# A last block product that accumulates onto U3, with new tile counts and scheduler margins, in a four-layer graph network on one core

## The chip, the cores and the metric

The kernel runs on one core of one Trainium2 chip. The metric is the device time of one execution in microseconds. The core has five engines that run side by side: TensorE (PE, matmuls; PEld is its weight load), VectorE (DVE), ScalarE (ACT), GpSimd (POOL) and SyncE (SP), whose queue here issues all transfers between memory and the on-chip buffers. Matmul results go to PSUM, which has eight banks; DVE and ACT read them from there.

## What is computed

Four graph layers follow one another, each closed by a residual sum and a layer norm. All data are fp32; `x` is 128 graphs x 64 nodes x 512 features. Cut to what matters:

```python
# layer 0
y = x @ w;  s = y @ a
A = s[..., :, None] + s[..., None, :];  A = tanh(A / 8) * 8;  A = where(A >= 0, A, 0.1 * A)
A = exp(A) * adj;  A = A / A.sum(-1) * adj.sum(-1)
x = layernorm(x + A @ x @ w)
# layer 1
weight = adj * exp(query @ key.T);  x = layernorm(x + weight / weight.sum(2) @ value)
# layer 2
w = scale * mask * sum(q * (adj @ k), -1);  x = layernorm(x + softmax(w) * (x @ Wv))
# layer 3
h = layernorm(relu(hypergraph_conv(x, adj, W1, b1)));  x = layernorm(x + hypergraph_conv(h, adj, W2, b2) + x)
```

`hypergraph_conv` multiplies by the weights and gathers along the graph's edges twice. What costs time are the dense products with weight matrices of 512x512 (layers 0 to 2), 512x1024 and 1024x512 (layer 3), for 8192 rows.

## The kernel before

**Tiling.** The 8192 rows are cut into 64 tiles of 128 rows, two graphs in each; two tiles make a group (`GT`), so there are 32 groups, and two groups make a pair (`SG`). Work inside one graph (gathers, scores) uses TensorE divided into 64x64 or 128x64 tiles, since a graph has 64 nodes; products with weights use the whole array.

**Seven products instead of eight.** Each dense product is done by a Strassen-Winograd scheme on 2x2 blocks. Of the left side A, sums s0 to s3 are made on DVE (`side_sums`); of the weights B, sums t1 to t4 are made once (`combine`) and stored. The order in which the seven right sides are stored and streamed is `USE` (L516). `products_of` (L949 on) does seven products in two standing PSUM banks (0 and 1) and two further banks: bank 0 takes A11 B11, then s1 t2 on top of it, which gives U2; then s2 t3 on top, which gives U3. Bank 1 takes s0 t1 and then s3 B22. A12 B21 and A22 t4 each go to a bank of their own. `first` moves a bank to the result block, `more` adds it to one; the callers give both as functions (`scaled_into`, `plain_into`, `z_into`, and a pair inside `run_rest`). C22 takes U3, and C21 is U3 plus the product A22 t4, taken from its own bank.

**Seven times seven.** The first weight product of layer 3 does the scheme on two levels (`forty_nine_products`, L1097), for a pair of groups at a time. `inner_products` (L1053) does one inner seven in two banks `x_` and `y_`: `times` issues a product, `into` moves columns of a bank into the result tile `f`. `use` adds the outer results into the blocks of h.

**Buffers.** Tiles are of few kinds with a fixed number each (L326 on): `x` 7 (activations of a group), `k4` 14 (left sides, sums and intermediate results of 1024 columns), `ring` 8 (weights on the way in), `adj` 10, `kept` 9, `e` 7, `col` 40, `bank` 8 (PSUM). Two kinds hold no memory and only limit how many are under way: `product` 3 (sevens) and `inner` 2.

**Order of the work.** Nothing runs in the order in which it is written. Every operation is recorded with its engine, an estimated cost, what it reads and writes, and a key (`Order.add`). `Order.run` is a list scheduler: it walks an own clock, and on each engine starts the ready operation with the smallest key whose tiles are free. The resulting order of each engine is then emitted and pinned; on the chip, engines wait for one another by semaphores. So all instructions have line L1471. Constants steer it:

- `BASE`, `EARLY`, `LEAD`, `PREPARED`: keys of groups, steps and the preparation of weights;
- `LATENCY`, `TO_PE`: how long after an operation's end another engine is taken to see it; for PE, `TO_PE` comes on top;
- `TURN`, `FAR`, `NEAR`, `ENOUGH` in `choose`: when PE is turned between the whole array ("whole") and a divided one ("quarters", "columns");
- `BLOCK`, `REST`: a divided matmul is let in only if the one 64 matmuls earlier began at least `REST` ns before;
- `AHEAD`, `TOGETHER`: how far transfers may run ahead, and how strongly the pieces of one weight are asked for together.

Of the kernel before, what the change touches and what calls it, by code (L numbers as in the profile page):

```python
# [28 lines left out]
APART = 4  # L29

BASE = [
    0.0, 1.743, 3.111, 5.432, 10.971, 14.755, 19.549, 23.249, 27.849, 31.549, 36.149, 39.849, 44.449, 48.149, 52.749, 56.449,
    61.049, 64.749, 69.349, 73.049, 77.649, 81.349, 85.949, 89.649, 94.249, 97.949, 102.549, 106.249, 111.542, 113.859, 117.859, 118.633,
]
RESIDENT = ("m1", "m2")
APART_3A = (0, NG // SG - 1)
LEAD = [0.325, -0.58]
PREPARED = [-5.214, 7.399, 8.218, 12.615, 11.711, -0.62]
PIECE = 1024
EPS = 1e-5  # L40
TINY = 1.1754944e-38
# [26 lines left out]
class Order:  # L68
    LATENCY = {"PE": 210, "DVE": 125, "ACT": 140, "POOL": 120, "SP": 2200}
    AGAIN = {"PE": 0, "DVE": 115, "ACT": 115, "POOL": 120}  # L70
    TO_PE = 100
    BYTES_PER_NS = 300
    UNDERWAY = 8
    TURN, TURN_DIVIDED = 145, 60

    NEAR = 0.5
    FAR = 5.712
    ENOUGH = 48

    EARLY = [2.22, 0.626, 0.0, 0.0, 0.0, -0.394, 0.0, 1.328, 0.0, 0.456, -0.17, -0.03, -0.766, -0.36, -1.408, -0.964]  # L80

    BLOCK, REST = 64, 3500
    AHEAD = 3.5
    TOGETHER = 1.0

    def __init__(self, slots):
        self.slots = {kind: list(range(n))[::-1] for kind, n in slots.items()}
# [200 lines left out]
def kernel(  # L288
# [34 lines left out]
    def kind(name, n, *shape, space=None):  # L323
        kinds[name] = [(space or sbuf).tile([P, *shape], FP, name=f"{name}{i}") for i in range(n)]

    kind("x", 7, GT, D)  # L326
    kind("k4", 14, PIECE)
    kind("ring", 8, PIECE)
    kind("h", 2, GT, DH)
    kind("k2", 2, D)  # L330
    kind("adj", 10, CT, N)
    kind("kept", 9, CT, N)
    kind("bh", 2, CT, N + 2)
    kind("e", 7, GT, N)
    kind("col", 40, 16)
    kind("bank", 8, D, space=psum)
    kinds["product"] = [None] * 3
    kinds["inner"] = [None] * 2

    order = Order({k: len(v) for k, v in kinds.items()})  # L340

# [171 lines left out]

    USE = ("b11", "t1", "b21", "t2", "b22", "t4", "t3")  # L516
    HALF = PIECE // 2

    def combine(b, t, n):
# [429 lines left out]
    def products_of(sides, pieces, across=False):  # L949


        going = Buf("product")
        pairs = [[Buf("bank") for _ in range(2)] for _ in sides]
        deep, wide = ("deep" in sides[0][0], "wide" in sides[0][0])
        chunks = KH // 2 if deep else KC // 2
        width = PIECE // chunks if deep or wide else D // 2
        pieces = iter(pieces)

        def times(of, ps, left, piece, view, start=True, also=(), gate=()):
            token = pairs[of][ps] if isinstance(ps, int) else ps  # L960

            def emit():
                l, b, o = left[1](), view(), token.t
                if across:
                    for c in range(2):
                        for k in range(chunks):
                            nc.tensor.matmul(o[:, ts(c, P)], b[:, k, ts(c, P)], l[:, k, :],
                                             start=start and k == 0 and c == 0,
                                             stop=k == chunks - 1, skip_group_check=True)
                else:  # L970
                    for k in range(chunks):
                        nc.tensor.matmul(o[:, :width], l[:, k, :], b[:, k, :], start=start and k == 0,
                                         stop=k == chunks - 1, skip_group_check=True)

            pe(w_pe(P, 2 * chunks) if across else w_pe(width, chunks), [left[0], piece, going, *gate], [token, *also], emit,
               matmuls=2 * chunks if across else chunks)
            return (token, going), lambda: token.t[:, :width]

        def all_times(ps, left, start=True, opens=False):
            piece, view = next(pieces)  # L980
            for of, (a, s, first, more) in enumerate(sides):
                yield first, more, times(of, Buf("bank") if ps is None else ps, left(a, s), piece, view, start,
                                         *(at_once if opens and of == 0 else ()))

        at_once = [b for pair in pairs[1:] for b in pair], [side[1][i][0] for side in sides[1:] for i in range(4)]
        for first, more, p in all_times(0, lambda a, s: a["11"], opens=True):
            first("11", *p)
        for first, more, p in all_times(1, lambda a, s: s[0]):
            first("22", *p)
        for first, more, p in all_times(None, lambda a, s: a["12"]):  # L990
            more("11", *p)
        for first, more, p in all_times(0, lambda a, s: s[1], False):
            first("12", *p)
        for first, more, p in all_times(1, lambda a, s: s[3], False):
            more("12", *p)
        for first, more, p in all_times(None, lambda a, s: a["22"]):
            first("21", *p)
        for first, more, p in all_times(0, lambda a, s: s[2], False):
            more("22", *p)
            more("21", *p)  # L1000

    def block_views(b, view):

# [8 lines left out]
    def scaled_into(at, f, own, n, sums):  # L1012


        def add(k, token, ps, last):
            dst = at[k]
            t = own.start + int(k[0]) - 1
            c = 2 * (int(k[0]) - 1) + int(k[1]) - 1
            dve(n + 40 + 70 * last, [*token, f, dst[0]], [dst[0], *([sums[c]] if last else [])], lambda: nc.vector.scalar_tensor_tensor(
                dst[1](), ps(), f.t[:, t : t + 1], dst[1](), ALU.mult, ALU.add,  # L1020
                **({"accum_out": sums.t[:, c : c + 1]} if last else {})), NOW)

        return lambda k, token, ps: add(k, token, ps, False), lambda k, token, ps: add(k, token, ps, True)

    def plain_into(b):

# [26 lines left out]
    def inner_products(raw, room, at, which, pieces, f, width):  # L1053


        going, x_, y_ = Buf("inner"), Buf("bank"), Buf("bank")
        raw_tok, raw_view = raw

        def side(k):
            if k in KEYS:  # L1060
                return raw_tok, lambda: raw_view(k)
            return room[int(k)], lambda: at(int(k))[:, which]

        def times(bank, i, k, start=True):
            piece, view = next(pieces)
            token, left = side(k)

            def emit():
                nc.tensor.matmul(bank.t[:, ts(i, width)], left(), view()[:, 0], start=start, stop=True, skip_group_check=True)

            pe(w_pe(width), [token, piece, going], [bank, *([y_] if k == "11" else [])], emit, matmuls=1)

        def into(cells, bank, i, n=1, first=False):
            n *= width
            dst = lambda: f.t[:, cells[0] * width : cells[0] * width + n]
            src = lambda: bank.t[:, i * width : i * width + n]
            if first:
                act(n, [bank], [f[cells]], lambda: nc.scalar.copy(dst(), src()), NOW)
            else:
                dve(n, [bank, f[cells]], [f[cells]], lambda: nc.vector.tensor_add(dst(), src(), dst()), NOW)  # L1080

        times(x_, 1, "11")
        times(x_, 0, "0", False)
        into([1, 2], x_, 0, 2, True)
        times(y_, 0, "12")
        times(x_, 1, "1", False)
        times(x_, 0, "3", False)
        into([0], x_, 1, 1, True)
        into([0], x_, 0)
        times(y_, 1, "22", False)  # L1090
        times(x_, 1, "2", False)
        into([3], x_, 1, 1, True)
        into([1], x_, 1)
        into([2, 3], y_, 0, 2)


    def forty_nine_products(xT, a, s, pieces, width, use):  # L1097
# [28 lines left out]
            return (of["tokens"], lambda k: of[k]()[:, m]), room, at, m  # L1126

        pieces = iter(pieces)
        for name in ("1", "5", "2", "6", "3", "4", "7"):
            raw, room, at, m = prepared_side(name)  # L1130
            f = Buf("k4", 4)
            inner_products(raw, room, at, m, pieces, f, width)
            use(name, f)
# [213 lines left out]
    def run_rest(n):  # L1347
# [15 lines left out]
        def h_block(r, j):  # L1363
            return hs[r][block_cells(j)], lambda: hs[r].t.rearrange("p t d -> p (t d)")[:, ts(j, DH)]
# [14 lines left out]
        def use(name, f_):  # L1379
            f = kept[name] = f_, lambda: f_.t  # L1380
            if name == "2":
                add(h_block(0, 0), kept["1"], f)
            elif name == "6":
                add(f, kept["1"], f, pool)
                add(h_block(0, 1), f, kept["5"])
            elif name == "3":
                add(h_block(0, 1), h_block(0, 1), f)
            elif name == "7":
                add(f, kept["6"], f, pool)
                add(h_block(1, 0), f, kept["4"])  # L1390
                add(h_block(1, 1), f, kept["5"])

        def by_part(v):
            return v.rearrange("p (i n) -> p i n", n=DH // 4)
# [147 lines left out]
```

## Time and profile before

| | |
|---|---|
| median of 3 runs | 2155.4 us (2155.09 to 2163.58) |
| profiled execution | 2158.28 us, its span 2156.5 us |
| granted TensorE clock | 0.997 |
| matmul records on PE | 21427 |
| ring<-3a, loads of 512 KB | 196, 4.9 us from issue to landing |
| ring<-v, loads of 512 KB | 189, 3.6 us from issue to landing |

The span is the time from the first to the last instruction of one profiled execution. Names of tiles stand without their numbers: `bank<-ring,k` is a matmul of a weight in `ring` with a left side in a `k` tile, `bank<-k,m` one with the weights that stay on the chip, `bank<-kept,h`, `bank<-kept,x`, `bank<-e,x` and `bank<-k,e` are the products inside graphs. A shape such as `128*128 128x256` gives the part of the array and then the output. An fp32 matmul leaves two records on PE and two weight loads on PEld; a transpose leaves one of each. DVE reads banks in these groups:

```profile
L1471 DVE SCALAR_TENSOR_TENSOR x<-bank,col,x 128x256 f32<-128x256 f32 x768 | 355.3, 480 | 274.9 <-PE bank L1471 259.1 <-issue 7.9 <-ACT k L1471 4.7
L1471 DVE TENSOR_TENSOR k<-bank,k 128x256 f32<-128x256 f32 x580 | 233.9, 420 | 161.0 <-PE bank L1471 112.0 <-ACT k L1471 42.5 <-ACT x L1471 0.5
...
L1471 DVE TENSOR_TENSOR k<-bank,k 128x512 f32<-128x512 f32 x98 | 66.8, 684 | 13.6 <-PE bank L1471 9.8 <-ACT k L1471 3.3
```

A row of groups gives the line, engine and operation, then out<-in, the shapes and the count; after the bar the busy time in us and the mean of one in ns; after the second bar the idle time before them and what ended most of it.

### The profile page before, as it was taken

The page shows a single profiled execution, that of the slowest core. Times are in us where ns is not written, and L with a number is a line of the kernel's source. Part 1 is how long each engine was busy: PE and PEld are TensorE (multiplying, and loading weights), DVE is VectorE, ACT ScalarE, POOL GpSimd, SP SyncE. Part 2 cuts the span into 40 slices and gives each one's busy share as a digit, 9 for nine tenths or more (in the row PEclk, how much of TensorE's full clock was granted, in tenths as well). Part 3 has the DMA queues.
Part 4 walks back from the last instruction along what each step waited for, and adds up shares of the span by engine and source line. Part 5 has one row for each costly group of instructions (what it writes and reads, how often), then busy time and mean ns, then how long its engine had stood idle before and what let it go on. Part 6 is the DMA issues. An engine that isn't in the chain of part 4 may idle for free.

```text
span 2156.5 us, 53957 instructions
## 1 busy us (share of the span) xinstructions
PE 2118.2 (98%) x21427; PEld 1833.8 (85%) x21427; DVE 1480.0 (69%) x4346; ACT 1195.4 (55%) x2698; POOL 457.5 (21%) x434
## 2 busy tenths in 40 slices
PE   8999999999999999999999999999999999999998
PEld 4897788888888898888888888898888888888875
DVE  5766876675686857668586685867768586765754
ACT  2544755464564645557464574645657365664554
POOL 1211330212211212121122211122121221212220
PEclk9999999999999999999999999999999999999999
DMA  8788873663655546456463555536465454645455
GB/s 270 257 310 288 298 268 116 219 212 116 204 177 209 188 147 212 144 205 209 162 204 135 200 191 200 193 127 228 152 209 194 170 198 136 209 161 186 159 189 184
DMA packets 166315, 422.36 MB, mean 196 GB/s; under 512 B 34928, under 2 KB 52528, under 8 KB 166064
## 3 DMA queue, kind: packets, MB, share of 16 engines
q1 hardware_dynamic: 166064, 418.92, 57.5%
q8 instruction: 169, 2.77, 0.5%
q14 instruction: 82, 0.67, 0.1%
HBM read 382.77 MB, written 36.08 MB: 194 GB/s over the span
## 4 chain that ended last, share of the span: by engine, by line
PE 95%; DMA 2%; ACT 1%; issue 1%; DVE 1%; SPq 0%; POOLq 0%; DVEq 0%; ACTq 0%
PE bank L1471 95%; DMA ring<-v 1%; ACT k L1471 1%; DMA adj<-mask_rows 1%; DVE k L1471 0%; ACT h L1471 0%; SPq L1471 0%; DMA ring<-3a 0%; DMA k<-in_wk_dram 0%; DVE x L1471 0%; DVE col L1471 0%; ACT e L1471 0%; ACT x L1471 0%; DVE ring L1471 0%; ACT m L1471 0%
## 5 line engine op out<-in xcount | busy, mean ns | idle before, releaser
L1471 PE MATMUL bank<-ring,k 128*128 128x256 f32 (+1 forms) x4940 | 1185.8, 388 | 7.9 <-ACT k L1471 4.8
L1471 PEld LDWEIGHTS bank<-ring,k 128*128 128x128 f32 x4940 | 903.3, 190 | 163.7 <-issue 22.9
L1471 ACT COPY k<-bank 128x512 f32<-128x512 f32 (+1 forms) x934 | 425.6, 483 | 425.5 <-PE bank L1471 370.1
L1471 DVE SCALAR_TENSOR_TENSOR x<-bank,col,x 128x256 f32<-128x256 f32 (+1 forms) x832 | 398.9, 500 | 277.8 <-PE bank L1471 261.8
L1471 PEld LDWEIGHTS bank<-k,m 128*128 128x128 f32 x3584 | 435.1, 192 | 15.2 <-ACT k L1471 2.4
L1471 PE MATMUL bank<-k,m 128*128 128x128 f32 x3584 | 442.7, 275 | 0.0
L1471 DVE TENSOR_TENSOR k<-bank,k 128x256 f32<-128x256 f32 (+1 forms) x678 | 295.0, 459 | 174.7 <-PE bank L1471 121.8
L1471 ACT ACTIVATE k<-x,col 128x512 f32<-128x512 f32 x256 | 183.9, 720 | 244.5 <-DVE col L1471 232.6
L1471 POOL TENSOR_TENSOR col<-col,mhalf 128x2 f32<-128x2 f32 (+1 forms) x161 | 111.6, 694 | 950.3 <-DVE col L1471 419.0
L1471 ACT ACTIVATE x<-x,col,col 128x512 f32<-128x512 f32 x256 | 198.4, 812 | 67.0 <-DVE col L1471 66.9
L1471 PE MATMUL bank<-ring,h 128*128 128x256 f32 x1024 | 233.0, 380 | 0.0
L1471 PEld LDWEIGHTS bank<-ring,h 128*128 128x128 f32 x1024 | 192.0, 190 | 26.3 <-issue 1.0
L1471 DVE TENSOR_TENSOR k<-k 128x256 f32<-128x256 f32 (+1 forms) x349 | 151.6, 454 | 47.0 <-ACT k L1471 44.2
L1471 DVE TENSOR_TENSOR k<-k,k 128x256 f32<-128x256 f32 (+3 forms) x361 | 174.4, 494 | 0.8
L1471 POOL TENSOR_TENSOR x<-x,bv_b 128x512 f32<-128x512 f32 x64 | 81.7, 1285 | 262.1 <-DVE col L1471 198.9
L1471 POOL TENSOR_TENSOR k<-k,b3b_b 128x512 f32<-128x512 f32 x64 | 80.4, 1270 | 201.2 <-DVE k L1471 148.2
L1471 PEld LDWEIGHTS bank<-k,k 128*64 128x64 f32 (+1 forms) x2112 | 77.9, 140 | 39.3 <-issue 27.0
L1471 PE MATMUL bank<-k,k 128*64 128x64 f32 (+1 forms) x2112 | 105.6, 238 | 5.5 <-DMA k<-in_wk_dram 5.1
L1471 ACT ACTIVATE k<-bank,u_c 128x128 f32<-128x128 f32 x256 | 85.9, 366 | 42.1 <-PE bank L1471 40.5
L1471 POOL TENSOR_TENSOR k<-k,k 128x1024 f32<-128x1024 f32 (+1 forms) x31 | 72.0, 2323 | 141.8 <-DVE k L1471 107.7
L1471 DVE TENSOR_TENSOR h<-k,k 128x1024 f32<-128x1024 f32 (+1 forms) x88 | 89.9, 1025 | 16.8 <-POOL k L1471 8.2
L1471 DVE TENSOR_SCALAR col<-col 128x2 f32<-128x2 f32 (+2 forms) x402 | 78.7, 199 | 24.4 <-ACT k L1471 18.0
(102 smaller groups left out, 1628.9 us busy)
## 6 DMA issues: line engine op xcount, KB each, us to landing
ring<-3a SPq DMA_DIRECT2D x196, 512.0 KB, 4.9
ring<-v SPq DMA_DIRECT2D x189, 512.0 KB, 3.6
ring<-3b SPq DMA_DIRECT2D x126, 512.0 KB, 4.6
ring<-w SPq DMA_DIRECT2D x93, 512.0 KB, 4.2
x<-in_x_dram SPq DMA_DIRECT2D x32, 512.0 KB, 6.3
ring<-v SPq DMA_DIRECT2D x63, 256.0 KB, 4.3
out_dram<-x SPq DMA_DIRECT2D x31, 512.0 KB, 6.4
ring<-w SPq DMA_DIRECT2D x31, 256.0 KB, 4.7
```

Of the source, the lines that this page charges most:

```text
L1471: made = f(*args, **kwargs)
```

## The change

The order of the last two products of a seven is exchanged, at both levels. s2 t3 makes U3 in bank 0, and `more` adds it to C22. Then A22 t4 accumulates in the same bank on top of U3, which makes C21 there, and `first` moves it. Before, C21 was written from the bank of A22 t4 and U3 was added to it. So one move out of PSUM is left out in each seven, and the last product has to wait until U3 has been read. In the inner sevens the bank `y_` now holds one product instead of two, and in `use` the block C21 of the outer level is the sum of results 4 and 7. `USE` and the streaming order follow. In `scaled_into` the running sum for the layer norm is taken by the write to C21 as well, since it is now the block's last.

Beside this the tile counts and the scheduler's constants are changed.

```diff
 BASE = [
-    0.0, 1.743, 3.111, 5.432, 10.971, 14.755, 19.549, 23.249, 27.849, 31.549, 36.149, 39.849, 44.449, 48.149, 52.749, 56.449,
...
+    0.0, 1.743, 3.111, 5.372, 10.971, 14.755, 18.98, 22.38, 27.28, 30.68, 35.58, 38.98, 43.88, 47.28, 52.18, 55.58,
...
-LEAD = [0.325, -0.58]
-PREPARED = [-5.214, 7.399, 8.218, 12.615, 11.711, -0.62]
+LEAD = [2.505, -0.294]
+PREPARED = [-3.906, 7.537, 8.271, 13.522, 12.862, -0.62]
...
-    TO_PE = 100
+    TO_PE = 300
...
-    FAR = 5.712
-    ENOUGH = 48
-
-    EARLY = [2.22, 0.626, 0.0, 0.0, 0.0, -0.394, 0.0, 1.328, 0.0, 0.456, -0.17, -0.03, -0.766, -0.36, -1.408, -0.964]
-
-    BLOCK, REST = 64, 3500
-    AHEAD = 3.5
-    TOGETHER = 1.0
+    FAR = 6.79728
+    ENOUGH = 28.88843999999999
+
+    EARLY = [2.22, 0.626, 0.0, -0.759, 0.0, -0.394, 0.0, 1.328, 0.0, 1.09, 0.384, -0.03, -0.766, -0.36, -1.408, -0.964]
+
+    BLOCK = 64
+    REST = 4500
+    AHEAD = 4.2
+    TOGETHER = 0.7
...
-    kind("x", 7, GT, D)
-    kind("k4", 14, PIECE)
+    kind("x", 6, GT, D)
+    kind("k4", 18, PIECE)
...
-    kind("adj", 10, CT, N)
-    kind("kept", 9, CT, N)
+    kind("adj", 6, CT, N)
+    kind("kept", 6, CT, N)
...
-    kind("e", 7, GT, N)
-    kind("col", 40, 16)
+    kind("e", 4, GT, N)
+    kind("col", 28, 16)
     kind("bank", 8, D, space=psum)
-    kinds["product"] = [None] * 3
-    kinds["inner"] = [None] * 2
+    kinds["product"] = [None] * 2
+    kinds["inner"] = [None] * 3
...
-    USE = ("b11", "t1", "b21", "t2", "b22", "t4", "t3")
+    USE = ("b11", "t1", "b21", "t2", "b22", "t3", "t4")
...
-        for first, more, p in all_times(None, lambda a, s: a["22"]):
-            first("21", *p)
         for first, more, p in all_times(0, lambda a, s: s[2], False):
             more("22", *p)
-            more("21", *p)
+        for first, more, p in all_times(0, lambda a, s: a["22"], False):
+            first("21", *p)
...
-        return lambda k, token, ps: add(k, token, ps, False), lambda k, token, ps: add(k, token, ps, True)
+        return lambda k, token, ps: add(k, token, ps, k == "21"), lambda k, token, ps: add(k, token, ps, True)
...
-        times(y_, 1, "22", False)
+        into([2], y_, 0)
         times(x_, 1, "2", False)
-        into([3], x_, 1, 1, True)
         into([1], x_, 1)
-        into([2, 3], y_, 0, 2)
+        times(x_, 1, "22", False)
+        into([3], x_, 1, 1, True)
...
-        for name in ("1", "5", "2", "6", "3", "4", "7"):
+        for name in ("1", "5", "2", "6", "3", "7", "4"):
...
-                add(h_block(1, 0), f, kept["4"])
                 add(h_block(1, 1), f, kept["5"])
+            elif name == "4":
+                add(h_block(1, 0), f, kept["7"])
```

More of the change, by code (lines that the diff above doesn't have):

```diff
@@ L31 @@
 BASE = [
-    0.0, 1.743, 3.111, 5.432, 10.971, 14.755, 19.549, 23.249, 27.849, 31.549, 36.149, 39.849, 44.449, 48.149, 52.749, 56.449,
-    61.049, 64.749, 69.349, 73.049, 77.649, 81.349, 85.949, 89.649, 94.249, 97.949, 102.549, 106.249, 111.542, 113.859, 117.859, 118.633,
+    0.0, 1.743, 3.111, 5.372, 10.971, 14.755, 18.98, 22.38, 27.28, 30.68, 35.58, 38.98, 43.88, 47.28, 52.18, 55.58,
+    60.48, 63.88, 68.78, 72.18, 77.08, 80.48, 85.38, 88.78, 93.68, 97.08, 101.98, 105.38, 110.213, 112.471, 117.658, 118.432,
 ]
@@ L1089, in inner_products @@
         into([0], x_, 0)
-        times(y_, 1, "22", False)
+        into([2], y_, 0)
         times(x_, 1, "2", False)
+        into([1], x_, 1)
+        times(x_, 1, "22", False)
         into([3], x_, 1, 1, True)
-        into([1], x_, 1)
-        into([2, 3], y_, 0, 2)
     def forty_nine_products(xT, a, s, pieces, width, use):
```

## The prediction

> **What bounds the kernel now.** First the page: busy shares, and the chain that ended last.
>
> ```profile
> PE 2118.2 (98%) x21427; PEld 1833.8 (85%) x21427; DVE 1480.0 (69%) x4346; ACT 1195.4 (55%) x2698; POOL 457.5 (21%) x434
> ...
> PE 95%; DMA 2%; ACT 1%; issue 1%; DVE 1%; SPq 0%; POOLq 0%; DVEq 0%; ACTq 0%
> ```
>
> TensorE is busy for 98% of 2156.5 us and carries 95% of the chain. The vector engine, from which the change takes work, idles for 31% and holds 1% of the chain. So I ask only what the change does to the stream of matmuls. What could still be saved there is next, in the waits of PE:
>
> ```profile
> PE bank L1471 <- issue: 12.8, 9, 3.7
> PE bank L1471 <- DMA k<-in_wk_dram: 5.1, 1, 5.1
> PE bank L1471 <- ACT k L1471: 4.9, 5, 1.9
> PE bank L1471 <- ACT e L1471: 4.5, 3, 3.7
> ```
>
> The largest item, nine stops of 12.8 us, waits for no buffer and no engine. The others stand at the start and the end. Waits under 0.15 us are not listed, so I read the timeline of PE; one stretch gives nearly all prices:
>
> ```profile
> 999.49 0.81 PE L1471 MATMUL bank<-ring,k 128*128 128x256 f32 x3
> 1000.24 1.15 PE L1471 MATMUL bank<-k,k 128*64 128x64 f32 x32
> 1001.32 1.16 PE L1471 MATMUL bank<-kept,h 64*64 64x64 f32 x64
> 1002.41 1.13 PE L1471 MATMUL bank<-ring,k 128*128 128x256 f32 x4
> 1003.38 0.28 PE L1471 MATMUL bank<-row_of,e 128*128 128x2 f32 x2
> ...
> 1010.43 1.63 PE L1471 MATMUL bank<-kept,h 64*64 64x64 f32 x96
> 1011.99 0.70 PE L1471 MATMUL bank<-ring,k 128*128 128x256 f32 x2
> ```
>
> Starts are to be compared, not durations, since matmuls overlap. A record on the whole array (128*128, 256 columns) starts 0.216 us after the one before. From whole to divided the start comes at 1000.24 instead of 999.49 + 3 x 0.216 = 1000.14: 0.10 lost. 64 records on 64*64 tiles last 1.09 to the next whole matmul, 96 last 1.56: 0.47 for 32, so 1.09 holds 0.15 that is no work. The next whole matmuls need 0.97 for four (0.86 of work): 0.10 more. One trip from whole to divided and back costs 0.35 us, a step between two divided shapes 0.15.
>
> Now a stop:
>
> ```profile
> 1263.50 1.09 PE L1471 MATMUL bank<-k,e 64*64 64x512 f32 x8
> 1264.41 1.46 PE L1471 MATMUL bank<-kept,h 64*64 64x64 f32 x88
> 1266.91 0.34 PE L1471 MATMUL bank<-kept,h 64*64 64x64 f32 x8 [1.03 <-issue]
> ```
>
> Eight records of one group come 1.25 us after the 88 before them. The DMA part of the page says what is fetched there:
>
> ```profile
> q8 instruction: 169, 2.77, 0.5%
> ```
>
> 169 packets of 16 KB bring PE's 42,854 recorded instructions, some 254 each: 64 fp32 matmuls of four instructions. The 128 matmul records before this stop began within 3.8 us; with the stop the block took 5.1. A block of 64 matmuls that is done faster than about 5 us outruns its fetch.
>
> And a short wait:
>
> ```profile
> 975.42 1.05 PE L1471 MATMUL bank<-k,m 128*128 128x128 f32 x8
> 976.51 0.70 PE L1471 MATMUL bank<-ring,k 128*128 128x256 f32 x2
> ```
>
> Eight records at 0.112 end at 976.32; the next starts 0.19 late, behind an addition of DVE, and the one after it 0.10 late again.
>
> **What the skill says.** TensorEngine Tiling (Array Packing), Key Properties: changing the tiling mode drains TensorE. The trace agrees: 0.35 us a trip. Runtime: NRT & Kernel Launch, Instruction fetch mechanics: instructions come in blocks of 256, the next fetched while one runs, the cost mostly hidden. The block size agrees; hidden it is not in nine places. TensorE: Matmul & The Clock Gate, Step-by-step: matmuls keep program order, only weight loads are pulled ahead, so a matmul that waits holds every later one. PSUM — Partial Sum Buffer, The four PSUM rules: a synchronised read in the middle of an accumulation group is allowed, which the new last link needs. The first bank of the kernel before is already read that way, so the trace has the case.
>
> **The change, part by part.** I compared the order that the two sources give on each engine.
>
> *Evacuations.* Removed on DVE: 96 scaled additions (128x256, 480 ns: 46 us), 96 plain ones (420 ns: 40 us), and 98 of 512 columns (684 ns) that shrink to 256 (26 us). DVE falls by some 112 us, ACT stays. On the path this is worth nothing: DVE's idle 31% covers it. Bytes, DMA count (1,017 rows on SP) and PE's work stay (10,970 matmuls become 10,966).
>
> *New wait.* The last product of a seven now waits until DVE has read U3 from the bank, at 196 places of the top level (six sevens for each of 32 groups, and four more in layer 3a) and 98 inner ones. Behind the waiting matmul stands all of PE. Price: 0 if enough other matmuls stand between. I laid the starts above along both orders. Links "matmul, read, matmul into the same bank" that continue a sum grow from 329 to 515, but those with under 0.9 us of PE work between fall from 20 to 0, and the trace shows links with 0.86 us between on time within 0.01. I take 0, with bounds 0 and +12 (a third of the 294 late by 0.12).
>
> *More turns.* Trips to divided tiles rise from 126 to 162, steps between divided shapes fall from 65 to 59: 36 x 0.354 - 6 x 0.148 = +11.9 us. Nothing hides this; every trip is PE's own time. FAR, ENOUGH and the longer REST split the divided runs: 66 runs of 48 matmuls become 60, runs of 16 or fewer rise from 12 to 49.
>
> *Fetch stops.* REST 4500 demands 4.5 us for any 64 matmuls before another divided one, against 3500. Cutting both orders into blocks of 256 instructions, I find 13 blocks below 5.1 us now, short by 14.9 in sum (measured 12.8); afterwards 8, short by 2.7. I take -10, with bounds -12.8 (all gone) and -6 (fetches meet full DMA queues).
>
> *Wider margins.* TO_PE 300 moves each consumer later in the order. In a clean period (910 to 1040 us; a pair of groups takes 130) short waits sum to 0.70 us, four of the five behind DVE or the restart after it. They recur in some 12 periods: 8.4 us. Weight loads behind small adjacency DMAs add 2.0 (six waits of 0.14 to 0.75 us on ring<-v). In the new order four tight chains a period become one, and no weight load stands behind those small DMAs. Of 10.4 us I take 6.5; bounds -10 and 0.
>
> *Start and end.* The first 40 us hold the same matmuls in nearly the same order. At the end one addition of 0.48 follows the last matmul in place of two, with one product between link and read: -0.5. PREPARED and LEAD shift the preparation: 0 +- 3.
>
> *Tiles.* k4 18 for 14, products under way 2 for 3, inner 3 for 2, smaller other kinds: no price of their own; they act through the order, which I have counted.
>
> Sum: +11.9 - 10 - 6.5 - 0.5 = -5.1 us. The profiled execution took 2158.28 (span 2156.5), the median of the runs is 2155.4. The sum is a difference, so I subtract it from the median: 2150.3, forecast 2150 us, -0.25%.
>
> **The rivals.**
> A, the sum above: no change within 0.5%, 2150. For it: every price comes from a repeated stretch. Chance 0.60.
> B, all waits that margins can reach go: fetch -12.8, short waits -10.4, the waits at start and end (4.9 + 4.5) by half, -4.7, the end -0.5: +11.9 - 28.4 = -16.5, 2139. For it: the tight chains are nearly gone. Against: the start's waits follow DVE's own queue, which is the same there. Chance 0.27, with those cases of A's spread below 2144.6.
> C, slower: the drained stream. The new last link, at 294 places, becomes the wait that ends last where DVE holds one more queued instruction than the order assumes. One such addition lasts 0.42 to 0.48, the slack past 0.86 is small, and each late start costs 0.10 more for the restart. If a third of the links lose 0.15 and that restart, 98 x 0.25 = +24 on A: 2174. It decides against the forecast from 64 such links (16 us) on. Against: none is under 0.9 us, and DVE has 112 us less to do. Chance 0.13.
> D, the fetch stops stay: the shorter blocks still outrun full queues, -3 instead of -10: 2157, also no change; inside A's chance.
>
> **How the numbers follow.** What a measurement can tell from no change is 0.5%, 10.8 us: 2144.6 to 2166.2. Faster 0.27 (B), same 0.60 (A and D), slower 0.13 (C). The ends of the unknown costs give A itself 2142 to 2162. To leave out no more than 2 in 10 the range goes to 2138 (B) and 2164.
>
> **What would show it.** Right: 162 trips in PE's timeline and about 0.35 us for each; "issue" waits of PE down from 12.8 to some 3 us; the period of the steady part, 130.2 us now, shorter by 0.1; DVE busy near 1368 us, PE still at 98%. Wrong: PE waits for DVE x or DVE k above 5 us (C); a sum of issue waits still above 8 (D); trips that cost clearly less than 0.35, as would be seen where a short divided run stands between whole matmuls (then B).

## The result, and the profile after

| 12 runs each, same chip | median | lowest to highest |
|---|---|---|
| before | 2158.66 us | 2154.53 to 2163.62 |
| changed | 2159.26 us | 2155.14 to 2166.51 |

The ratio is 1.0005, 95% interval 0.9991 to 1.0019: no difference that can be measured. 2150 was forecast. The time lies inside the range that was given (2138 to 2164), but the gain of 5 us (ratio 0.9976) lies outside the interval.

The profiled executions stand at 2158.28 us (before) and 2155.14 us (changed, the fastest of its 12 runs), so the profile after shows the changed kernel a little better than it usually is. Its page, busy shares and chain:

```profile
PE 2120.1 (98%) x21419; PEld 1829.5 (85%) x21419; DVE 1403.6 (65%) x4150; ACT 1204.8 (56%) x2698; POOL 460.0 (21%) x434
...
PE 92%; DMA 4%; SPq 1%; ACT 1%; DVE 1%; issue 0%; POOLq 0%; ACTq 0%; DVEq 0%
```

PE is busy for 98% as before, but its share of the chain fell from 95% to 92%, and that of DMA rose from 2% to 4%. The waits of PE say which transfer it is (what was waited for, us in total, times, longest):

```profile
PE bank L1472 <- DMA ring<-3a: 8.6, 9, 1.4
PE bank L1472 <- ACT k L1472: 7.5, 5, 3.0
PE bank L1472 <- DMA k<-in_wk_dram: 4.5, 2, 4.1
PE bank L1472 <- DVE e L1472: 1.9, 2, 1.7
```

The stops for instructions ("issue", 12.8 us before) are gone from the list. At its head stands a wait of which the list of before has one, of 0.7 us:

```profile
PE bank L1471 <- DMA ring<-3a: 0.7, 1, 0.7
```

PE now waits nine times for a load of layer 3a's factors. In the chain of waits the nine loads are asked for between 564 and 1740 us, in nine of ten pairs of groups that follow one another; here are two:

```profile
1085.38 6.01 DMA ring<-3a
1091.39 0.04 issue
1091.43 124.77 PE bank L1472 x1309
1216.20 0.02 issue
1216.22 6.32 DMA ring<-3a
```

Each line is a start, a length and what ran. The load is asked for at 1085.38 and PE can only go on at 1091.4; then 125 us of matmuls, and the same again. The load takes 6 us, when the median of the 196 loads on the page is 4.5. SP's timeline shows what is asked for around it:

```profile
1082.13 4.04 SPq L1472 DMA_DIRECT2D ring<-3a  x4
1086.22 1.08 SPq L1472 DMA_DIRECT2D adj<-in_adjT_dram  x2
1087.34 1.32 SPq L1472 DMA_DIRECT2D ring<-3a  x1
```

Four loads of 512 KB are issued within 4 us, 2 MB in all, and a fifth soon after. The first two land in 3.3 and 3.2 us, the third, at 1085.38, in 6.0, the fourth in 7.0. That their standing so close is the reason is not shown; e11 below has the same bunch with other landings. By the order of the sources the tile that the third load fills is released by its last reader 4.99 us of PE work before the load's own use; in the trace PE comes to a stand at 1090.32, 4.94 us after the load was asked for. That is enough for a landing of 4.5 us and not for one of 6.

PE's timeline gives the length of a pair of groups and the price of a trip:

```profile
1089.50 0.39 PE L1472 MATMUL bank<-e,same 128*128 128x128 f32 x2
...
1091.43 1.56 PE L1472 MATMUL bank<-ring,k 128*128 128x256 f32 x6 [1.11 <-DMA ring<-3a]
...
1107.36 0.60 PE L1472 MATMUL bank<-ring,k 128*128 128x256 f32 x2
1107.89 0.69 PE L1472 MATMUL bank<-k,k 128*64 128x64 f32 x16
1108.51 1.16 PE L1472 MATMUL bank<-e,x 64*64 64x64 f32 x64
1109.60 0.69 PE L1472 MATMUL bank<-k,k 128*64 128x64 f32 x16
...
1220.34 0.39 PE L1472 MATMUL bank<-e,same 128*128 128x128 f32 x2
```

Two whole matmuls are 0.43 of work, the divided one starts 0.53 after the first: 0.10 lost, as before the change. 64 records on 64*64 tiles again last 1.09 with a step to another divided shape. The trips have kept their price. From 1089.50 to 1220.34 a pair takes 130.84 us, where it took 130.2 before, not 0.1 less as forecast. One pair of the changed kernel goes without the wait. Its load, asked for at 826.06, lands in 4.4 us:

```profile
830.18 0.38 PE L1472 MATMUL bank<-e,same 128*128 128x128 f32 x2
830.40 0.60 PE L1472 MATMUL bank<-ident,x 128*128 128x128 f32 x4
830.84 1.46 PE L1472 MATMUL bank<-ring,k 128*128 128x256 f32 x6
...
959.65 0.38 PE L1472 MATMUL bank<-e,same 128*128 128x128 f32 x2
```

The weight matmul follows the transposes without a stop, and the pair takes 129.47 us.

### The profile page after: what moved, and what is told of

It is laid out like the page before. It is cut to its first block, busy times and chain, and to the rows that moved or that the text cites. A ratio compares the mean times of both kernels' runs of the same rounds, so it can differ in the third digit from the quotient of the medians.

```text
span 2153.2 us, 53735 instructions
## 1 busy us (share of the span) xinstructions
PE 2120.1 (98%) x21419; PEld 1829.5 (85%) x21419; DVE 1403.6 (65%) x4150; ACT 1204.8 (56%) x2698; POOL 460.0 (21%) x434
## 4 chain that ended last, share of the span: by engine, by line
PE 92%; DMA 4%; SPq 1%; ACT 1%; DVE 1%; issue 0%; POOLq 0%; ACTq 0%; DVEq 0%
PE bank L1472 92%; DMA ring<-3a 3%; SPq L1472 1%; ACT k L1472 1%; DMA adj<-in_adjT_dram 0%; DMA k<-in_wk_dram 0%; ACT h L1472 0%; DMA x<-in_x_dram 0%; DMA 3a<-k 0%; DMA ring<-in_wv_dram 0%; DMA adj<-mask_rows 0%; DVE h L1472 0%; DVE col L1472 0%; DVE x L1472 0%; DVE k L1472 0%
## 5 line engine op out<-in xcount | busy, mean ns | idle before, releaser
L1472 PE MATMUL bank<-ring,k 128*128 128x256 f32 x4940 | 1191.1, 388 | 16.0 <-DMA ring<-3a 8.6
L1472 ACT COPY k<-bank 128x256 f32<-128x256 f32 (+1 forms) x934 | 428.0, 483 | 437.7 <-PE bank L1472 426.8
L1472 DVE SCALAR_TENSOR_TENSOR x<-bank,col,x 128x256 f32<-128x256 f32 (+1 forms) x736 | 367.6, 504 | 301.3 <-PE bank L1472 291.6
L1472 DVE TENSOR_TENSOR k<-bank,k 128x256 f32<-128x256 f32 x582 | 235.6, 420 | 193.3 <-PE bank L1472 127.4
L1472 DVE TENSOR_TENSOR k<-k,k 128x256 f32<-128x256 f32 (+3 forms) x361 | 165.1, 465 | 0.8
L1472 PE MATMUL bank<-k,k 128*64 128x64 f32 (+1 forms) x2112 | 110.0, 239 | 4.6 <-DMA k<-in_wk_dram 4.5
L1472 DVE TENSOR_SCALAR col<-col 128x2 f32<-128x2 f32 (+2 forms) x402 | 84.0, 214 | 33.1 <-ACT k L1472 23.4
```

Source lines behind the costliest of these rows:

```text
L1472: made = f(*args, **kwargs)
```

## The experiments

Times taken on different chips or at different times differ by some us, so what is compared is the ratio to the kernel before, run beside each on the same chip. "Trips" are turns of PE from whole to divided tiles, by the order of the source (the matmul records of the traces give the same counts); "issue" is PE's wait for instructions in the profiled run.

| run | what it is | trips | issue, us | median, us | ratio (95%) |
|---|---|---|---|---|---|
| changed | | 162 | 0 | 2159.3 | 1.0005 (0.9991 to 1.0019) |
| e1 | products and tiles, constants of before | 147 | 4.7 | 2155.7 | 0.9980 (0.9972 to 0.9989) |
| e2 | tiles and constants, products of before | 165 | 5.8 | 2226.1 | 1.0313 (1.0287 to 1.0339) |
| e3 | changed, REST 3500 | 187 | 1.6 | 2172.4 | 1.0057 (1.0037 to 1.0076) |
| e4 | changed, half of the 3a loads | 162 | 0 | 2143.9 | 0.9923 (0.9901 to 0.9944) |
| e5 | before, half of the 3a loads | 126 | 9.8 | 2162.1 | 1.0006 (0.9997 to 1.0014) |
| e6 | tiles alone | 146 | 17.7 | 2190.3 | 1.0122 (1.0104 to 1.0140) |
| e7 | e1, TOGETHER 0.7 | 137 | 7.7 | 2165.3 | 1.0023 (1.0013 to 1.0032) |
| e8 | e1, REST 4500 | 138 | 1.6 | 2147.3 | 0.9941 (0.9927 to 0.9956) |
| e9 | e4, NEAR 0 | 196 | 0 | 2183.6 | 1.0104 (1.0083 to 1.0126) |
| e10 | e8, tiles in the order they came free | 138 | 1.5 | 2146.6 | 0.9939 (0.9917 to 0.9960) |
| e11 | changed, tiles in the order they came free | 162 | 0 | 2150.6 | 0.9949 (0.9932 to 0.9966) |
| e12 | e7, half of the 3a loads | 137 | 7.5 | 2163.4 | 1.0032 (1.0020 to 1.0045) |

**Are the late loads real (e4, e5)?** The load brings half, all instructions and their order stay:

```diff
-                      lambda t_=t_, src=src, n=n, width=width: nc.sync.dma_start(
-                          out=t_.t[:, : n * width], in_=src.t[:, : n * width]),
+                      lambda t_=t_, src=src, m=n * width // (2 if which == "3a" and order.group else 1): nc.sync.dma_start(
+                          out=t_.t[:, :m], in_=src.t[:, :m]),
```

> The changed kernel, but after the first groups every load of layer 3a's factors (ring<-3a) brings only half its columns; the other half of the tile keeps what it held, so part of layer 3a is computed from old factors. All instructions and their order are unchanged. Theory 1 (in the changed kernel PE waits once a period for a ring<-3a load, 1.2 to 1.6 us at seven places, 8.6 us in its PE waits plus restarts): these waits vanish and the time falls by 8 to 11 us, to about 2149. Rival (these waits only stand in for something else that is late at the same places, or differ from run to run): same as the changed kernel within 3 us, 2156 to 2162.

The ratio fell from 1.0005 to 0.9923, by 0.8% or some 18 us (with both intervals, 12 to 23). Between the two profiled executions, of which the changed kernel's is its fastest, it is 11.3 (2155.14 to 2143.83). The waits are gone, and in the timeline of e4 a pair of groups is

```profile
1085.32 0.38 PE L1472 MATMUL bank<-e,same 128*128 128x128 f32 x2
1085.54 0.60 PE L1472 MATMUL bank<-ident,x 128*128 128x128 f32 x4
1085.98 1.46 PE L1472 MATMUL bank<-ring,k 128*128 128x256 f32 x6
...
1214.79 0.39 PE L1472 MATMUL bank<-e,same 128*128 128x128 f32 x2
```

129.47 us long. Four transposes from 1085.54 take 0.44 and the weight matmul starts at 1085.98, on time; in the changed kernel it stood still there. The 129.47 are those of the changed kernel's own pair without the wait. So of the 130.84, 1.37 is the wait with its restart, and nine such pairs make 12.3 us, about the 11.3 between the profiled executions.

The same cut in the kernel before:

> The kernel before with the same cut as e4: after the first groups each ring<-3a load brings only half its columns, so part of layer 3a is computed from old factors; the order is that of before. It tells how much of the time of before is waiting for these loads. Theory 1 (late loads of weights are what the change added; the profile of before shows 2 us of them): before minus 2 to 8 us. Rival (before waits for them as much as the changed kernel does, which fell by some 15 us with the same cut): before minus 12 us or more, and then these loads do not explain why the change brought nothing.

Nothing moved: 1.0006, so neither number came, not even the 2 to 8 us of theory 1. The kernel before hardly waits for these loads, so the wait is the change's own.

**Who brings what (e1, e2, e6)?** e1 takes the tiles and the products of the change, of which the core is

```diff
-    kind("x", 7, GT, D)
-    kind("k4", 14, PIECE)
+    kind("x", 6, GT, D)
+    kind("k4", 18, PIECE)
...
-        for first, more, p in all_times(None, lambda a, s: a["22"]):
-            first("21", *p)
...
+        for first, more, p in all_times(0, lambda a, s: a["22"], False):
+            first("21", *p)
```

and leaves `BASE`, `EARLY`, `LEAD`, `PREPARED`, `TO_PE` and all of `FAR` to `TOGETHER` as they were.

> The changed products and the new numbers of tiles, with every constant of the scheduler as before. By the order of the sources it has 147 trips from whole to divided tiles (126 before, 162 after), 45 steps between divided shapes (65 before), and 15 blocks of 256 PE instructions below 5.1 us (13 before). Theory 1 (PE's stream of matmuls sets the time, so only trips, fetch stops and late weight loads count): turns +4.4 us against before, fetch stops +3 to +5, so about 2166 us, and issue waits of PE at 14 to 18 us. Theory 2 (the relief of DVE by the products is worth something of itself): at or below before, 2159 or less. Theory 3 (the new last link of a product exposes DVE): PE waits for DVE x or DVE k above 5 us, and 2170 or more.

Theory 1 failed here: 0.998 of before, not 1.002. The trips in its trace are the 147 that were counted; the fetch stops are 4.7 us where 14 to 18 were expected, which is the size of the miss. Theory 3 fails too: PE waits for DVE x 1.9 us and for DVE k 0.6. The time is that of theory 2, but it does not show theory 2's reason, since the fetch stops fell as well.

e2 takes the constants and tiles without the products, e6 the tiles alone:

> The products of before, with all the changed constants of the scheduler and the new numbers of tiles. 165 trips, 44 steps between divided shapes, 9 blocks below 5.1 us, short by 8.6 us. Theory 1: turns +10.7 us against before, fetch stops -4 to -9, a late ring<-3a load in each period (+6 to +12): 2162 to 2172 us, close to the changed kernel or a little above it; the turns of the change are then the constants' and not the products'. Theory 2 (the products matter): clearly slower than the changed kernel, by 15 us or more, with DVE waits on PE. Theory 3 (the products' last link costs): faster than the changed kernel.

> The kernel before with nothing changed but the numbers of tiles. 146 trips, 59 steps between divided shapes: +6.2 us of turns on before, 9 blocks of 256 instructions under 4.2 us as before (8). Against e1 (the same tiles and the changed products, 2155.7 us, 147 trips, 45 steps) it tells what the products are worth with the tiles and constants fixed. Theory 1 (only PE's stream counts, products are worth nothing): e1 plus 2 us, about 2158. Theory 2 (with few tiles the relief of DVE is needed, as e2 at 2226 us suggests): 2170 us or more with waits of PE for DVE or ACT.

Both came out far slower, as their second theories had it. The waits of PE in e2:

```profile
PE bank L1472 <- DVE col L1472: 23.5, 8, 2.9
PE bank L1472 <- ACT x L1472: 12.6, 2, 10.8
```

and in e6:

```profile
PE bank L1471 <- issue: 17.7, 11, 2.9
PE bank L1471 <- ACT k L1471: 6.5, 7, 1.9
PE bank L1471 <- DVE k L1471: 4.9, 4, 4.0
```

With the new numbers of tiles the products are worth 1.4% with the old constants (1.0122 of e6 less 0.9980 of e1, some 31 us) and 3.1% with the new ones (e2 less the changed kernel, some 66 us). In e2 the largest wait is for DVE, eight times, 2.9 us each. The name `col` is that of the small operation that came last: before PE goes on at 1009.72, for instance, DVE works without a gap, 3.43 us of it in two operations on `h`. These stops cost more than their length. At each of the eight, the trace has the granted clock at 0.5 for 3.4 or 6.8 us about the moment PE goes on (0.50 from 1009.8 to 1013.2), and six matmul records of 128 columns then take 1.57 us where eight took 1.06 just before. Over the whole run the clock was 0.984 in e2 and 0.997 in the changed kernel; on 2236 us that is some 29 us, an estimate. The late ring<-3a load that theory 1 expected in each period did not come: four waits, 2.7 us.

In e6, 13 us are more fetch stops than in e1 (17.7 against 4.7), 4.3 are DVE k (4.9 against 0.6), and the rest is spread over waits that were not told apart; that PE would wait for DVE or ACT explains little of it. With the numbers of tiles of before the scheduler finds no order for the changed products, so there is no kernel with the products alone.

**REST and the fetch stops (e3, e8).**

> The changed kernel with REST back at 3500. 187 trips instead of 162, 64 steps between divided shapes, 19 short blocks (short by 13.6 us, 3.4 in the changed kernel). Theory 1: +9.6 us for the turns and +8 to +12 for fetch stops, which return as issue waits of PE of 10 us or more: 2177 to 2181 us. Rival (a fetch stop costs only where the queues are full, or was never REST's doing): issue waits stay below 2 us and the time is 2169.

25 more trips and 5 more steps are 9.6 us, and the ratio is 0.0052 above the changed kernel's, 11 us: the rival's number. The fetch stops did not return; REST 3500 does not bring them of itself. That turns and stops fill the 11 us is in part chance, because something else went: e3 waits for ring<-3a loads 1.0 us and not 8.6. Other waits came in their place (DVE k 4.3 us, ACT k 9.4 for 7.5), so that the listed waits of PE grew by 2.5 in all, from 25.7 to 28.2, between profiled executions that differ by 14.8.

```diff
-    BLOCK, REST = 64, 3500
+    BLOCK = 64
+    REST = 4500
```

> e1 with REST 4500 for 3500. 138 trips for 147, 49 steps for 45, PE's priced stream 2.6 us shorter than in e1, 2 blocks under 4.2 us for 10. Theory 1: 2.6 us of turns and most of e1's 4.7 us of fetch stops go, no weight load is late: 2147 to 2151 us, faster than both kernels. Rival (REST does nothing for fetch stops, as e3 suggests, where REST 3500 had 1.6 us of them): 2153 us.

This one line on e1 gives 0.9941: faster than both kernels. The priced stream is 2.6 us shorter and the issue waits fall from 4.7 to 1.6; some 3 us more than these two went, not told apart. (How far such a sum moves by itself can be seen in the kernel before and e5, which have the same order on PE: 12.8 and 9.8.)

**One more constant (e7, e12).**

> e1 (changed products and tiles, constants of before) with one more constant of the change, TOGETHER 0.7 for 1.0: the later loads of one product are asked for nearer to their use and not with the first. 137 trips for 147, PE's priced stream 1.4 us shorter than in e1. Theory 1 (this constant brings the late ring<-3a loads): these waits appear in PE's waits, once or more a period, and the time is 2160 to 2170. Rival (the late loads come from another constant or from the new numbers of tiles): 2153 to 2156.

The time is in the band of theory 1, but its profiled run has only 2.1 us of ring<-3a waits. So the loads were cut there too:

> e7 (changed products and tiles, constants of before but TOGETHER 0.7; 2165.3 us, 1.0023 of before) with half of each ring<-3a load left out after the first groups, so that part of layer 3a is computed from old factors; the order of all instructions is that of e7. It asks whether e7's 9.6 us over e1 are late ring<-3a loads, of which its profile showed only 2.1 us. Theory 1 (they are): 0.993 to 0.998 of before, at or below e1's 0.998. Rival (TOGETHER costs something else, as it reorders PE's work): within 3 us of e7, 1.001 to 1.004.

1.0032: the loads are not the cause, and theory 1 is wrong about TOGETHER. It reorders PE's work, and the order is dearer by 0.4%; 3 us of that are fetch stops (7.7 against 4.7), the reason for the rest stays open. No constant that was tried alone brings the late load of 3a: e1 has 0.7 us of such waits, e7 2.1, e8 (REST 4500) 0.2, the changed kernel 8.6. But e3, the changed kernel with REST back, has only 1.0. So it takes REST 4500 together with another of the changed constants; which one stays open.

**The price of turns, again (e9).**

> e4 (the changed kernel with half of each ring<-3a load left out, so that part of layer 3a is computed from old factors; 2143.9 us) with NEAR 0 for 0.5, which makes the scheduler turn to divided tiles sooner: 196 trips instead of 162, 58 steps between divided shapes instead of 59, the same matmuls, no block of 256 instructions below 4.2 us. Theory 1 (a trip costs 0.35 us of PE's own time wherever it stands): 34 x 0.354 - 0.15 = +11.9 us, 2154 to 2158 us. Rival (turns hide beside other stalls, and the change's 36 more trips cost it little): 2144 to 2149.

The time rose by 40 us instead of 12. The waits of PE say why:

```profile
PE bank L1472 <- ACT h L1472: 12.9, 8, 1.6
```

NEAR 0 brought a matmul too near to the ACT operation on `h` that it reads, eight times. The 28 us above the turns hold this wait; what else they hold was not told apart. The run says nothing against the price of a turn, but it does not measure it either.

**Which tile is taken (e10, e11).** The last tile to come free was the first to be given out; here it is the last:

```diff
-    b.slot = self.slots[b.kind].pop()
+    b.slot = self.slots[b.kind].pop(0)
```

> e8 (changed products and tiles, constants of before but REST 4500; 2147.3 us) with tiles and banks given out in the order in which they came free, not the last one first. The order of instructions on PE is the same, only which bank and tile each uses differs, so matmuls find their bank read earlier: links of matmul, DVE or ACT and matmul with little between (below 0.9 us) weigh 1.7 us instead of 4.7 by the order of the source. Theory 1: 1 to 4 us less, 2143 to 2147 us. Rival (these links are already hidden): 2147 within 1 us.

> The changed kernel with the same rule for tiles and banks as e10, the PE order unchanged. The ring has no spare tile when a load is placed, so the ring<-3a loads stand as near to their use as before. Theory 1 (the late ring<-3a loads set what is left): the same as the changed kernel within 3 us, 0.999 to 1.002 of before, ring<-3a waits of PE still some 8 us. Rival (short waits for banks cost the changed kernel as much): 4 us or more below it.

On e8 it gave nothing (0.9939 against 0.9941), on the changed kernel 0.6%, some 12 us: the rival's number, and theory 1 failed. But the profile does not bear out the rival's reason:

```profile
PE bank L1472 <- DMA ring<-3a: 3.0, 4, 1.3
```

The same loads are asked for in the same bunch and at the same distance from their use, but five of the nine waits are gone, 5.6 us. Between the profiled runs (2155.14, the changed kernel's fastest, and 2150.77) that is more than the whole fall. From 690 to 1610 us the third load of the bunch, which in the changed kernel took 5.0 us or more in seven of eight pairs, lands in 4.2 to 4.8 us in six of eight. Why it lands sooner is not settled; at a distance of 4.99 us that decides.

## Why the prediction missed

Step by step, between the profiled executions, which differ by -3.1 us:

- *Turns, +11.9:* right as far as it was measured. The counts are those of the trace (162 and 126), and the single prices are the same in it after the change. No run isolates the sum: in e3 and e9 other waits changed along with the trips.
- *Fetch stops, -10:* they are all gone, -12.8, the end of the bounds. The number was met, the reason given for it, REST, is mostly wrong, so this is luck in part. e1, with REST 3500, has 4.7 us of stops, and the changed kernel with REST back at 3500 has 1.6 (e3). Most of the 12.8 went with products and tiles together (the tiles alone have 17.7, e6); REST took 3.1 in e8. The threshold of 5.1 us was wrong too: e3 has 19 blocks below it, short by 13.6 us.
- *New last link, 0:* right. PE waits for DVE x and DVE k do not appear in the list after, and C with its +24 did not come.
- *Evacuations, worth nothing on the path, and tiles, no price of their own:* each wrong by itself. e6 shows that the tiles alone cost 1.2%, and e1 that the products pay this back and 0.2% more. An idle share of DVE of 31% was no proof that it is never late where tiles are few: in e2 PE waits 23.5 us for it. In the sum the two cancel, because they come as a pair; that was not foreseen. DVE's busy time fell by 76 us and not by 112: the 96 scaled additions less took 33.1 us off their row and not 46, and some small `col` operations took longer.
- *Wider margins, -6.5, bounds -10 and 0: this is the step that failed.* It asked of a weight load only whether it stood behind small adjacency transfers, found none that did, and counted the 2.0 us of late loads as saved. That a load could become late without such a neighbour was left out, and so was any loss: the bound ended at 0. In the new order one ring<-3a load per pair has 4.99 us between the release of its tile and its use, and it lands in 6. The distance alone would not have told it: the kernel before has one such load per pair at 5.2 us, which lands in 3.2 to 3.4 and is never waited for, and of the e2 loads at 4.2 to 4.4 most land in 3.2 to 3.9. The trace has nine such waits, 8.6 us in the fastest run where -2.0 was forecast; e4 puts the loads at up to 18 us by the medians.

  The other part of the step did come. The profiled -3.1 is +11.9 for turns, -12.8 for stops, +8.6 for loads, and -10.8 for all the rest, short waits, start and end together. This rest is not in the listed waits for DVE, ACT and the first load (15.4 us before, 17.1 after). The pairs show where it is: in the kernel before the two pairs without any listed wait, of the eight from 609 to 1650 us, take 129.3 and 129.2 us (from 740.39 and from 1390.92), the one without a wait after the change 129.47 with three trips more, 1.06 us. So some 0.8 us a pair went elsewhere, and 0.70 of short waits had been read.
- *A pair, 0.1 us shorter:* 0.6 longer. Without the late load it is 129.47 (e4, seven pairs in a row), 0.7 shorter than before, although it holds ten trips instead of seven.

Rival B, 2139 or 16.5 us below before, has the number that the change would have been worth without this wait: e4 stands 0.77% below before, some 17 us (an upper bound, since its cut takes other traffic off the queues too). It does not have the grounds: the waits at start and end did not fall by half. None of the rivals named a load of weights as the new wait.

The versions that beat both kernels are e8 (the products, the tiles and REST 4500, with the other constants as they were), 2147.3 us, 0.9941 of before; e10, which differs from it by nothing that can be measured; and e11, 0.9949.

## What to carry to other kernels

When a schedule is moved, lay the distance between the release of a buffer and the next use of what is loaded into it beside the measured landing time of that load, for every load of a period. Take the landing of loads that stand alike in their bunch and not the median: here the distance was 4.99, the median 4.5, and loads of one bunch landed in 3.2 to 7.0. A load whose distance lies inside that spread may be late, and e11 and e2 show that it need not be; give it a bound on the side of loss. And judge parts of a change that need each other only together: here the new numbers of tiles cost 1.2% with the products of before and nothing with the changed ones, and neither part shows its price alone.

## What the runs showed of the hardware

- A period without a late transfer repeats to the hundredth: seven pairs in a row take 129.47 us each in e4, and so does the one pair of the changed kernel without the wait (830.18 to 959.65).
- 512 KB loads land 4.5 us after their issue (median), 256 KB loads of e4 3.0 us. Of four that were issued within 4 us the first two took 3.3 and 3.2, the third 6.0 and the fourth 7.0. In eight pairs the fourth took 6.0 to 7.4 us in the changed kernel and 5.6 to 7.3 in e11, the third 4.4 to 6.3 and 4.2 to 6.1.
- The "issue" stops fit PE's instruction fetch: each of the 24 in the kernel before, e1 and e6 ends 1.2 to 1.6 us after a 16 KB packet of q8 has passed. The length of a block of 64 fp32 matmuls alone does not foretell a stop. By the order of the sources, blocks below 4.2 us number 8 (before), 10 (e1), 9 (e6), 2 (e8) and 0 (changed), and the traces have 9, 4, 11, 1 and 0 stops. The Trainium skill (Runtime: NRT & Kernel Launch, Instruction fetch mechanics) calls the cost of fetching mostly hidden; in e6 17.7 us of it were not.
- A stop of PE can come with a halved clock: at all eight stops of 2.9 us for DVE in e2 the granted clock is 0.5 for 3.4 or 6.8 us. Not every stop does so: in e6 PE stops 2.9 us for instructions, up to 1020.74, and from 1017 to 1028 the clock stays at 1.00.
